# A two-layer metaformer in one kernel: weight loads one per tick, filter products partly in single PSUM banks, tokens 38 ticks behind pixels, and new orders outside full ticks

## The chip, the cores and the metric

One core of a Trainium2 chip runs the kernel. The metric is the device time of one execution in microseconds (us), the median of three runs.

## The reference

Eight images of 128 x 128 pixels with 96 channels pass two layers. A layer adds a spectral filter, then a small quantised feed-forward:

```python
x_pre = scale * relu(ln(x) @ w1.T) ** 2 + bias                 # 192 channels
xf = rfft2(x_pre)
filt = stack of 3: complex resize of cw0, cw1, cw2 to (128, 65)
r = softmax(gate(mean of x, mean of relu(bn(x @ sp_w.T))))     # per image, 3 x 192
x = x + irfft2(xf * sum_s(filt[s] * r[s])) @ w2.T
x = x + ffn(ln(x))                                             # 96 -> 384 -> 96, fp8 products
```

## The kernel before

The work is cut into 256 groups per stage (2 layers x 8 images x 16 groups) and three stages, each a generator that yields between steps: **pixels** P (norm, first product, DFT along the width, result to a_d in DRAM), **frequencies** F (read a_d, DFT along the height, filter times gate, inverse, result to y_d), **tokens** S (read y_d, last inverse DFT, add x, norm, feed-forward, write). N is the norm's small steps, U the filter products of a layer (12 groups of 8 rows, `filters`), G the gate of an image.

A loop over ticks t, from -4 on, runs a table of (stage, step, ahead): step of group t - offset + ahead. The order of a table is the order in which instructions enter each engine's queue. There are five tables: RAMP (t under 15, pixels alone), RISE (to t = 37, pixels and frequencies), TICK (full, to 257), FALL (to 275, frequencies and tokens), TAIL (tokens alone). The offset of F is 19, that of S is 40. U runs at t = 3 to 14 for layer 0 and at t = 21 to 32 for layer 1. The steps, by engine:

- P: 0 SP load xt (L526); 1 DVE st (L465); 2 POOL xn (L536); 3 PE pt_a (L540); 4 ACT xT (L543); 5 PE pw0, 10 PE pw1 (L551); 6, 11 ACT r (L554); 7, 12 ACT xs (L557); 8, 13 POOL acc (L563); 9, 14 DVE sd (L569); 15, 16 PE pa0, pa1 (L578); 17, 19 ACT lo (L592); 18, 20 DVE at (L594, L595), 20 with the store to a_d (L598).
- F: 0 SP load al, ut (L679, L681); 1 POOL ut (L685); 2, 3 PE pf0, pf1 (L697); 4 px; 5, 10 PE py0, py1 (L731); 6, 7 ACT cf (L738); 8, 11 DVE pr (L755 to L759); 9, 12 POOL xf (L774); 13, 14 PE pz (L813, L821); 15 ACT zt (L828); 16 PE pi (L837); 17 ACT yo (L840); 18 DVE yt (L844) with the store to y_d (L853).
- S: 0 SP load v, xr (L862, L865); 1 PE ps_r (L871); 2 DVE xr (L880, L882); 3 DVE st; 4, 5 xn_c on ACT and DVE (L892, L898); 6 PE pt_c (L906); 7 ACT xq; for k = 0, 1, 2: 8+4k PE pm (L916), 9+4k ACT y (L919), 10+4k DVE a (L922), 11+4k h (L926); 20 PE po (L933); 21, 22 o (L948); 23 POOL y (L951) with the store.
- U: 0 PE ps_u (L292); 1 ACT copies (L308); 2 DVE copies (L306) with the store to u_d (L311).

PSUM's eight banks are three pairs (d0, d1, d2) and two single ones (s3, s4). A BANKS table per phase says in which of them a product lies (`bank2` gives a pair, `bank1` a single); a product waits until its bank's last product has been read. All loads and stores are issued by SP, in program order. Weights are loaded and converted by events at fixed ticks, after pixel step 9: among them the layer-0 token weights (L394 to L417) at 7 and 11, layer 1's filter source cw (`load_filters`, L283) at 16, its projection weights (L334 to L369) at 19 and 23. Until t = 36 the pool `us` holds what loading needs; then the tokens' pool `sb` takes that memory.

Of the kernel before, what the change touches and what calls it, by code (L numbers as in the profile page):

```python
# [76 lines left out]
    ("F", 12, 0), ("P", 5, 0), ("P", 13, -1), ("U", 0, 0), ("U", 1, 0), ("F", 13, 0),  # L77
    ("P", 1, 2), ("P", 14, -1), ("F", 8, 1), ("P", 6, 0), ("F", 9, 1), ("P", 15, -1),
    ("U", 2, 0), ("P", 16, -1), ("P", 17, -1), ("P", 18, -1), ("F", 14, 0), ("P", 19, -1),
    ("F", 10, 1), ("P", 7, 0), ("P", 20, -1), ("F", 0, 3), ("P", 8, 0), ("F", 15, 0),  # L80
    ("N", 0, 0), ("N", 1, 0), ("P", 0, 4), ("P", 9, 0), ("F", 1, 2), ("P", 10, 0),
    ("P", 11, 0), ("N", 2, 0), ("F", 16, 0), ("F", 2, 2), ("F", 17, 0), ("F", 3, 2),
    ("P", 12, 0), ("F", 4, 2), ("F", 11, 1), ("F", 5, 2), ("P", 2, 2), ("F", 6, 2),
    ("P", 3, 2), ("F", 7, 2), ("P", 4, 2), ("F", 18, 0),
# [3 lines left out]
    1: ((7, 0), (19, 1), (19, 2), (21, 3), (21, 4), (37, 5), (43, 6)),  # L88
    2: ((15, 7), (23, 8), (23, 9), (26, 10)),
# [3 lines left out]
    ("F", 7, 1), ("F", 0, 2), ("S", 6, 0), ("S", 0, 2), ("F", 18, -1), ("S", 1, 1),  # L93
    ("S", 7, 0), ("S", 15, -1), ("S", 16, -1), ("S", 8, 0), ("F", 8, 1), ("S", 23, -3),
    ("S", 9, 0), ("S", 2, 1), ("S", 3, 1), ("N", 0, 0), ("S", 20, -2), ("S", 21, -2),
    ("S", 10, 0), ("F", 12, 0), ("F", 1, 2), ("F", 13, 0), ("F", 9, 1), ("F", 10, 1),
    ("S", 17, -1), ("N", 1, 0), ("S", 11, 0), ("S", 12, 0), ("S", 13, 0), ("F", 14, 0),
    ("F", 2, 2), ("S", 18, -1), ("N", 2, 0), ("F", 3, 2), ("F", 15, 0), ("F", 16, 0),
    ("S", 4, 1), ("S", 5, 1), ("F", 4, 2), ("F", 5, 2), ("S", 22, -2), ("F", 17, 0),
    ("F", 6, 2), ("S", 19, -1), ("F", 11, 1), ("S", 14, 0),  # L100
# [20 lines left out]
    "ps_u0": 2, "ps_u1": 0, "pa0": 0, "pa1": 2, "pw0": 1, "pw1": 2, "pt_a": 1,  # L121
# [8 lines left out]
    "ps_u0": 2, "ps_u1": 1, "ps_g": 3, "ph": 4, "pl": 3, "pa0": 2, "pa1": 0, "pw0": 0,  # L130
    "pw1": 2, "pt_a": 2, "pf0": 0, "pf1": 2, "py0": 1, "py1": 1, "pz0": 3, "pz1": 4,
    "pi0": 3, "pi1": 4, "px": 3, "pg": 4,
}
FALL_BANKS = {
    "pf0": 0, "pf1": 2, "py0": 1, "py1": 1, "pz0": 3, "pz1": 4, "pi0": 4, "pi1": 3,
    "ps_r0": 3, "ps_r1": 4, "pt_c": 0, "pm0": 1, "pm1": 2, "pm2": 2, "po": 0, "px": 4,
}
TAIL_BANKS = {
    "ps_r0": 3, "ps_r1": 4, "pt_c": 1, "pm0": 1, "pm1": 2, "pm2": 2, "po": 0,
# [100 lines left out]
def metaformer_kernel(ctx: ExitStack, tc: tile.TileContext, x, cst, layers, out):  # L240
# [44 lines left out]
    def filters(i):  # L285

        l, n0 = i // NU, i % NU * UN
        pss = []
        for i in range(2):
            pss.append(bank2(f"ps_u{i}")[:NKW, :, : UN * UM])  # L290
        for i in range(M // UM):
            mm(  # L292
                pss[i // 2][:, i % 2, :].rearrange("p (n m) -> p n m", m=UM),
                kt["rw"][32 * i : 32 * i + NWS],
                cws[l][32 * i : 32 * i + NWS, :, n0 : n0 + UN].rearrange("p m n -> p n m"),
                start=True,
                stop=True,
            )
        yield
        u = us.tile([NKW, UN, M], F32, name="u", bufs=3)  # L300
        uv = u.rearrange("p n (i a m) -> p i a n m", a=2, m=UM)
        for i, ps in enumerate(pss):
            for a in range(2):
                o = ps[:, a, :].rearrange("p (n m) -> p n m", m=UM)
                if i:
                    nc.vector.tensor_copy(uv[:, i, a], o)  # L306
                else:
                    nc.scalar.copy(uv[:, i, a], o)  # L308
            if i:
                n1 = n0 if n0 < NHS else 64 + n0 - NHS  # L310
                nc.sync.dma_start(u_d[l][:, n1 : n1 + UN, :], u)  # L311
            yield
# [7 lines left out]
    temps = [{}, {}, {}]  # L320
# [13 lines left out]
    def projection_weights(l, p):  # L334
# [26 lines left out]
        temps[l]["cen"] = cen  # L361
        ps = bank1("ps_w")
# [9 lines left out]
    def other_weights(l, p):  # L372
# [3 lines left out]
        for i in range(2):  # L376
            nc.sync.dma_start(fc1s[i * SC : (i + 1) * SC], p["conv_fc1"][C:, :])
        nc.vector.memset(kept(l, "fc1g", [C, GK]), 0.0)
        nc.vector.memset(kept(l, "fc1s", [2 * SC, GK]), 0.0)
        nc.vector.memset(kept(l, "fc2", [GK, NS * M]), 0.0)  # L380
        nc.sync.dma_start(kept(l, "mlp_s", [GK, 1]), row(p["conv_mlp_scale"], GK))
        nc.sync.dma_start(kept(l, "mlp_b", [GK, 1]), row(p["conv_mlp_bias"], GK))
        dc = kept(l, "dc", [HH, 1])
        nc.sync.dma_start(dc, row(p["conv_soa1_bias"], HH))
        nc.sync.dma_start(wt["fc2"][:RHID], p["conv_fc2"])
        yield
        ps = bank1("ps_w")
# [6 lines left out]
    def token_weights(l, p):  # L394
        wt = wts[l]


        nc.sync.dma_start(kept(l, "w2a", [128, C]), p["conv_w2"][:128, :])
        nc.sync.dma_start(kept(l, "w2c", [128, C]), p["conv_w2"][64:, :])
        w2b = kept(l, "w2b", [128, C])  # L400
        nc.sync.dma_start(w2b[:64], p["conv_w2"][128:, :])
        nc.sync.dma_start(w2b[64:], p["conv_w2"][:64, :])
        f1, f2, b1, b2 = (
            load(l, f"{name}_f", shape, view)
            for name, shape, view in (
                ("f1", [C, HID], p["ffn_W1"]),
                ("f2", [128, HID // 128, C], p["ffn_W2"].rearrange("(k p) c -> p k c", p=128)),
# [673 lines left out]
```

## Time and profile before

| | |
|---|---|
| median of three runs | 4958.87 us (4958.15 to 4959.98) |
| the profiled execution | 4954.99 us, its span 4952.9 us |
| mean granted TensorE clock | 0.986 |
| busy: PE, PEld, DVE, ACT, POOL | 97%, 76%, 93%, 87%, 51% |
| moved by DMA | 1020.95 MB, 206 GB/s |

The profile is one execution. PE is TensorE's products, PEld its weight loads beside them, DVE VectorE, ACT ScalarE, POOL GpSimd, SP the queue that issues transfers. A busy share is an average over phases with different limits, so it is read phase by phase. Waits name the releaser that came last.

### The profile page before, as it was taken

The page shows a single profiled execution, that of the slowest core. Times are in us where ns is not written, and L with a number is a line of the kernel's source. Part 1 is how long each engine was busy: PE and PEld are TensorE (multiplying, and loading weights), DVE is VectorE, ACT ScalarE, POOL GpSimd, SP SyncE. Part 2 cuts the span into 40 slices and gives each one's busy share as a digit, 9 for nine tenths or more (in the row PEclk, how much of TensorE's full clock was granted, in tenths as well). Part 3 has the DMA queues.
Part 4 walks back from the last instruction along what each step waited for, and adds up shares of the span by engine and source line. Part 5 has one row for each costly group of instructions (what it writes and reads, how often), then busy time and mean ns, then how long its engine had stood idle before and what let it go on. Part 6 is the DMA issues. An engine that isn't in the chain of part 4 may idle for free.

```text
span 4952.9 us, 123961 instructions
## 1 busy us (share of the span) xinstructions
PE 4817.7 (97%) x44232; PEld 3749.4 (76%) x44232; DVE 4587.1 (93%) x13963; ACT 4321.2 (87%) x7107; POOL 2532.7 (51%) x1889
## 2 busy tenths in 40 slices
PE   7899999999999999999999999999999999999987
PEld 4577777777777777777777787777777777777753
DVE  7777999999999999999999999999999999998888
ACT  5555799999999999999999999999999999997887
POOL 3445455555555555555555555555555555554544
PEclk9999999999999999999999999999999999999987
DMA  5677788888788888888888887888888888887754
GB/s 156 189 189 198 209 214 215 215 213 214 212 217 213 215 216 214 214 213 218 213 213 216 212 216 211 218 214 214 214 213 216 213 215 214 215 209 183 204 149 127
DMA packets 917423, 1020.95 MB, mean 206 GB/s; under 512 B 75826, under 2 KB 848914, under 8 KB 916602
## 3 DMA queue, kind: packets, MB, share of 16 engines
q1 hardware_dynamic: 916810, 1013.04, 77.2%
q8 instruction: 352, 5.77, 0.5%
q14 instruction: 261, 2.14, 0.1%
HBM read 598.92 MB, written 413.84 MB: 204 GB/s over the span
## 4 chain that ended last, share of the span: by engine, by line
PE 90%; DVE 4%; ACT 2%; issue 1%; DMA 1%; POOL 0%; SPq 0%; POOLq 0%; DVEq 0%; ACTq 0%
PE pw L551 16%; PE py L731 14%; PE pz L821 9%; PE pf L697 8%; PE pi L837 7%; PE pa L578 7%; PE pm L916 6%; PE pz L813 6%; PE po L933 5%; PE pt_a L540 4%; PE ps_r L871 4%; PE pt_c L906 2%; PE ps_u L292 1%; DVE st L465 1%; DVE xr L882 0%
## 5 line engine op out<-in xcount | busy, mean ns | idle before, releaser
L774 POOL TENSOR_TENSOR xf<-pr 128x768 f32<-128x768 f32 x512 | 931.4, 1819 | 419.4 <-DVE pr L759 409.7
L551 PE MATMUL pw<-w,xT 97*128 97x240 f32 x4096 | 943.7, 374 | 5.0 <-DVE at L595 2.9
L731 PE MATMUL py<-k_fwd,al 128*128 128x128 f32 (+1 forms) x6208 | 802.3, 280 | 0.7 <-DVE mx L637 0.4
L919 ACT CAST y<-pm 128x1024 f16<-128x1024 f32 x768 | 756.7, 1017 | 43.6 <-PE pm L916 43.4
L551 PEld LDWEIGHTS pw<-w,xT 97*128 97x128 f32 x4096 | 743.6, 191 | 58.0 <-issue 11.2
L731 PEld LDWEIGHTS py<-k_fwd,al 128*128 128x128 f32 (+1 forms) x6208 | 744.9, 191 | 41.1 <-DVE pr L759 1.7
L563 POOL TENSOR_TENSOR acc<-acc,r 128x192 f32<-128x192 f32 x496 | 296.3, 597 | 935.6 <-ACT r L554 860.9
L926 ACT ACTIVATE h<-a 128x1024 fp8e5<-128x1024 f16 x726 | 769.9, 1060 | 0.9 <-DVE a L922 0.9
L951 POOL TENSOR_TENSOR y<-xr,o 128x768 f32<-128x768 f32 x256 | 422.1, 1649 | 674.4 <-DVE o L948 582.3
L554 ACT ACTIVATE r<-pw 128x960 f32<-128x960 f32 x512 | 497.5, 972 | 115.9 <-PE pw L551 115.3
L569 DVE TENSOR_TENSOR sd<-xs 128x384 f32<-128x384 f32 x1008 | 531.9, 569 | 6.0 <-PE pa L578 5.9
L755 DVE TENSOR_TENSOR pr<-py,cf 128x768 f32<-128x768 f32 x512 | 487.0, 951 | 40.9 <-PE py L731 28.2
L685 POOL TENSOR_TENSOR ut<-ut,rw 112x768 f32<-112x768 f32 (+1 forms) x256 | 472.7, 1846 | 61.0 <-DMA ut<-u_d 42.0
L697 PEld LDWEIGHTS pf<-k_rh,ut 48*128 48x128 f32 x6080 | 362.2, 189 | 153.7 <-issue 136.3
L916 PE MATMUL pm<-xq,f_q 96*128 96x512 fp8e5 x1536 | 435.3, 391 | 40.1 <-ACT y L919 16.4
L536 POOL TENSOR_TENSOR xn_a<-xt,n_rs 128x768 f32<-128x768 f32 x256 | 378.6, 1479 | 141.2 <-DVE n_rs L499 118.5
L557 ACT ACTIVATE xs<-r 128x768 f32<-128x768 f32 x512 | 436.7, 853 | 0.4
L909 ACT ACTIVATE xq<-pt_c 96x1024 fp8e5<-96x1024 f32 x256 | 261.3, 1021 | 198.3 <-PE pt_c L906 198.3
L697 PE MATMUL pf<-k_rh,ut 48*128 48x128 f32 x6080 | 411.5, 282 | 9.7 <-POOL ut L685 9.5
L892 ACT ACTIVATE xn_c<-xr,n_nb,n_rs 128x96 fp8e5<-128x96 f32 x1062 | 414.6, 488 | 0.0
L578 PE MATMUL pa<-sd,dft 64*64 64x384 f32 x4096 | 396.8, 497 | 8.3 <-ACT r L554 4.7
L738 ACT COPY cf<-pf 128x768 f32<-128x768 f32 x496 | 373.5, 802 | 32.0 <-PE pf L697 30.3
(131 smaller groups left out, 10108.2 us busy)
## 6 DMA issues: line engine op xcount, KB each, us to landing
a_d<-at SPq DMA_DIRECT2D x256, 768.0 KB
al<-a_d SPq DMA_DIRECT2D x1024, 192.0 KB
y_d<-yt SPq DMA_DIRECT2D x512, 192.0 KB
v<-y_d SPq DMA_DIRECT2D x256, 384.0 KB
ut<-u_d SPq DMA_DIRECT2D x256, 336.0 KB
xt<-in_x_dram SPq DMA_DIRECT2D x512, 96.0 KB
xr<-in_x_dram SPq DMA_DIRECT2D x256, 192.0 KB
mid<-y SPq DMA_DIRECT2D x256, 192.0 KB
```

Of the source, the lines that this page charges most:

```text
L551: mm(o, xT[:, 4 * a + 2 * i + j, :], wt["w1"], start=True, stop=True)
L554: nc.scalar.activation(r.rearrange("p a s c -> p a (s c)"), pw, AF.Relu)
L569: on.tensor_tensor(sd[:, e], xs[:, 0], xs[:, 1], op)
L578: mm(pa[64 * e : 64 * e + 64, p].rearrange("q (s m) -> q s m", m=M), wt["dft"][64 * p : 64 * p + 64, 64 * e : 64 * e + 64], sd[64 * p : 64 ...
L685: nc.gpsimd.tensor_tensor(ut[:, -n:], ut[:, -n:], _bc_mid(jb.rw, n), ALU.mult)
L697: mm(pf[:, i, t * 128 : (t + 1) * 128], utf[64 * i : 64 * i + NHS, c0 : c0 + 128], kt["rh"][64 * i : 64 * i + NHS, :], start=True, stop=True,)
L731: mm(py[p0:p1, t, e, :], alf[:, e, c0 + p0 : c0 + p1], f, start=True, stop=True)
L755: nc.vector.tensor_tensor(p0, yv, crb, ALU.mult)
L774: nc.gpsimd.tensor_tensor(xf.rearrange("p t e f -> p (t e) f"), pr[:, 0].rearrange("p t r k -> p t (r k)"), pr[:, 1].rearrange("p t r k -> ...
L916: mm(pm[:, s, :], fk, xq[:, s, :], start=True, stop=True)
L919: nc.scalar.copy(y16, pm)
L926: nc.scalar.activation(hk, a16, AF.Copy, saturate=False)
```

## The change

The tokens' offset becomes 38, so RISE ends at t = 35, TICK runs from 36, and TAIL ends two ticks sooner. `filters` puts two of its four products into one pair (ps_u) and the others into s3 and s4 (ps_v0, ps_v1); ACT copies the first two out, DVE the others, as before. The events are replaced by one generator, `background`, of which one piece runs per tick from t = 0: one or two small loads a piece; layer 0's token weights come at 12 to 14 and are converted at 16, cw of layer 1 comes at 17, layer 1's projection weights at 18 to 21, with their small steps at 22 and their product ps_w at 23. padding(1) moves from 34 to 36. RAMP, RISE, FALL and TAIL get new orders and, in part, other banks; TICK, GATE and BANKS stay.

```diff
 RISE = (
-    ("F", 12, 0), ("P", 5, 0), ("P", 13, -1), ("U", 0, 0), ("U", 1, 0), ("F", 13, 0),
-    ("P", 1, 2), ("P", 14, -1), ("F", 8, 1), ("P", 6, 0), ("F", 9, 1), ("P", 15, -1),
-    ("U", 2, 0), ("P", 16, -1), ("P", 17, -1), ("P", 18, -1), ("F", 14, 0), ("P", 19, -1),
-    ("F", 10, 1), ("P", 7, 0), ("P", 20, -1), ("F", 0, 3), ("P", 8, 0), ("F", 15, 0),
-    ("N", 0, 0), ("N", 1, 0), ("P", 0, 4), ("P", 9, 0), ("F", 1, 2), ("P", 10, 0),
-    ("P", 11, 0), ("N", 2, 0), ("F", 16, 0), ("F", 2, 2), ("F", 17, 0), ("F", 3, 2),
-    ("P", 12, 0), ("F", 4, 2), ("F", 11, 1), ("F", 5, 2), ("P", 2, 2), ("F", 6, 2),
-    ("P", 3, 2), ("F", 7, 2), ("P", 4, 2), ("F", 18, 0),
+    ("F", 7, 1), ("P", 1, 2), ("P", 0, 3), ("P", 13, -1), ("U", 0, 0), ("F", 12, 0),
+    ("P", 3, 1), ("P", 5, 0), ("N", 0, 0), ("U", 1, 0), ("P", 4, 1), ("F", 13, 0),
+    ("U", 2, 0), ("P", 14, -1), ("P", 6, 0), ("P", 15, -1), ("F", 8, 1), ("P", 16, -1),
+    ("P", 17, -1), ("F", 14, 0), ("P", 7, 0), ("P", 18, -1), ("F", 9, 1), ("P", 8, 0),
+    ("F", 10, 1), ("P", 19, -1), ("P", 20, -1), ("N", 1, 0), ("F", 15, 0), ("F", 11, 1),
+    ("P", 9, 0), ("F", 0, 3), ("P", 10, 0), ("P", 11, 0), ("F", 16, 0), ("F", 1, 2),
+    ("F", 2, 2), ("N", 2, 0), ("F", 3, 2), ("F", 17, 0), ("P", 12, 0), ("P", 2, 2),
+    ("F", 4, 2), ("F", 5, 2), ("F", 18, 0), ("F", 6, 2),
 )
 RISE_GATE = {
-    1: ((7, 0), (19, 1), (19, 2), (21, 3), (21, 4), (37, 5), (43, 6)),
-    2: ((15, 7), (23, 8), (23, 9), (26, 10)),
+    1: ((8, 0), (25, 1), (29, 2), (37, 3), (38, 4), (42, 5), (45, 6)),
+    2: ((7, 7), (24, 8), (30, 9), (32, 10)),
 }
 FALL = (
-    ("F", 7, 1), ("F", 0, 2), ("S", 6, 0), ("S", 0, 2), ("F", 18, -1), ("S", 1, 1),
-    ("S", 7, 0), ("S", 15, -1), ("S", 16, -1), ("S", 8, 0), ("F", 8, 1), ("S", 23, -3),
-    ("S", 9, 0), ("S", 2, 1), ("S", 3, 1), ("N", 0, 0), ("S", 20, -2), ("S", 21, -2),
-    ("S", 10, 0), ("F", 12, 0), ("F", 1, 2), ("F", 13, 0), ("F", 9, 1), ("F", 10, 1),
-    ("S", 17, -1), ("N", 1, 0), ("S", 11, 0), ("S", 12, 0), ("S", 13, 0), ("F", 14, 0),
-    ("F", 2, 2), ("S", 18, -1), ("N", 2, 0), ("F", 3, 2), ("F", 15, 0), ("F", 16, 0),
-    ("S", 4, 1), ("S", 5, 1), ("F", 4, 2), ("F", 5, 2), ("S", 22, -2), ("F", 17, 0),
-    ("F", 6, 2), ("S", 19, -1), ("F", 11, 1), ("S", 14, 0),
+    ("S", 14, -1), ("F", 0, 2), ("S", 6, 0), ("F", 17, -1), ("S", 1, 1), ("S", 19, -2),
+    ("S", 0, 2), ("F", 7, 1), ("S", 7, 0), ("F", 18, -1), ("F", 8, 1), ("S", 23, -3),
+    ("S", 2, 1), ("S", 15, -1), ("F", 12, 0), ("S", 3, 1), ("N", 0, 0), ("S", 20, -2),
+    ("S", 16, -1), ("S", 8, 0), ("S", 21, -2), ("S", 9, 0), ("S", 17, -1), ("S", 10, 0),
+    ("S", 18, -1), ("F", 1, 2), ("N", 1, 0), ("F", 9, 1), ("S", 11, 0), ("S", 12, 0),
+    ("F", 13, 0), ("F", 10, 1), ("S", 13, 0), ("N", 2, 0), ("F", 14, 0), ("S", 4, 1),
+    ("F", 2, 2), ("F", 15, 0), ("S", 5, 1), ("F", 3, 2), ("F", 4, 2), ("F", 16, 0),
+    ("S", 22, -2), ("F", 11, 1), ("F", 5, 2), ("F", 6, 2),
 )
 RAMP = (
-    ("P", 0, 4), ("U", 0, 0), ("U", 1, 0), ("P", 3, 2), ("P", 20, -1), ("P", 1, 4),
-    ("P", 7, 1), ("P", 13, 0), ("P", 4, 2), ("U", 2, 0), ("N", 1, -1), ("N", 0, 0),
-    ("P", 8, 1), ("P", 14, 0), ("N", 2, -1), ("P", 2, 3), ("P", 9, 1), ("P", 10, 1),
-    ("P", 15, 0), ("P", 16, 0), ("P", 11, 1), ("P", 5, 2), ("P", 17, 0), ("P", 18, 0),
-    ("P", 19, 0), ("P", 12, 1), ("P", 6, 2),
+    ("U", 0, 0), ("P", 0, 4), ("P", 13, 0), ("U", 1, 0), ("P", 20, -1), ("P", 7, 1),
+    ("P", 1, 4), ("U", 2, 0), ("P", 3, 2), ("P", 4, 2), ("P", 8, 1), ("N", 1, -1),
+    ("P", 14, 0), ("N", 0, 0), ("N", 2, -1), ("P", 2, 3), ("P", 9, 1), ("P", 10, 1),
+    ("P", 15, 0), ("P", 11, 1), ("P", 16, 0), ("P", 17, 0), ("P", 18, 0), ("P", 19, 0),
+    ("P", 5, 2), ("P", 12, 1), ("P", 6, 2),
 )
TAIL = (
...
)
 RAMP_BANKS = {
-    "ps_u0": 2, "ps_u1": 0, "pa0": 0, "pa1": 2, "pw0": 1, "pw1": 2, "pt_a": 1,
+    "pa0": 0, "pa1": 1, "pw0": 2, "pw1": 2, "pt_a": 1, "ps_u": 0, "ps_v0": 3, "ps_v1": 4,
 }
 BANKS = {
     "ps_g": 4, "ph": 3, "pl": 4, "pa0": 1, "pa1": 0, "pw0": 0, "pw1": 0, "pt_a": 0,
     "pg": 3,
 }
 RISE_BANKS = {
-    "ps_u0": 2, "ps_u1": 1, "ps_g": 3, "ph": 4, "pl": 3, "pa0": 2, "pa1": 0, "pw0": 0,
-    "pw1": 2, "pt_a": 2, "pf0": 0, "pf1": 2, "py0": 1, "py1": 1, "pz0": 3, "pz1": 4,
-    "pi0": 3, "pi1": 4, "px": 3, "pg": 4,
+    "ps_g": 3, "ph": 3, "pl": 3, "pa0": 2, "pa1": 0, "pw0": 0, "pw1": 2, "pt_a": 2,
+    "pf0": 0, "pf1": 2, "py0": 1, "py1": 1, "pz0": 3, "pz1": 4, "pi0": 3, "pi1": 4,
+    "px": 3, "pg": 3, "ps_u": 0, "ps_v0": 3, "ps_v1": 4,
 }
 FALL_BANKS = {
-    "pf0": 0, "pf1": 2, "py0": 1, "py1": 1, "pz0": 3, "pz1": 4, "pi0": 4, "pi1": 3,
-    "ps_r0": 3, "ps_r1": 4, "pt_c": 0, "pm0": 1, "pm1": 2, "pm2": 2, "po": 0, "px": 4,
+    "pf0": 0, "pf1": 2, "py0": 1, "py1": 1, "pz0": 3, "pz1": 4, "pi0": 3, "pi1": 4,
+    "ps_r0": 3, "ps_r1": 4, "pt_c": 0, "pm0": 1, "pm1": 2, "pm2": 0, "po": 2, "px": 4,
 }
 TAIL_BANKS = {
-    "ps_r0": 3, "ps_r1": 4, "pt_c": 1, "pm0": 1, "pm1": 2, "pm2": 2, "po": 0,
+    "ps_r0": 3, "ps_r1": 4, "pt_c": 0, "pm0": 0, "pm1": 2, "pm2": 2, "po": 1,
 }
...
     def filters(i):
         l, n0 = i // NU, i % NU * UN
-        pss = []
-        for i in range(2):
-            pss.append(bank2(f"ps_u{i}")[:NKW, :, : UN * UM])
+        pu = bank2("ps_u")
+        pss = [pu[:NKW, i, : UN * UM] for i in range(2)]
+        pss += [bank1(f"ps_v{i}")[:NKW, : UN * UM] for i in range(2)]
         for i in range(M // UM):
             mm(
-                pss[i // 2][:, i % 2, :].rearrange("p (n m) -> p n m", m=UM),
+                pss[i].rearrange("p (n m) -> p n m", m=UM),
                 kt["rw"][32 * i : 32 * i + NWS],
                 cws[l][32 * i : 32 * i + NWS, :, n0 : n0 + UN].rearrange("p m n -> p n m"),
                 start=True,
             )
         yield
         u = us.tile([NKW, UN, M], F32, name="u", bufs=3)
-        uv = u.rearrange("p n (i a m) -> p i a n m", a=2, m=UM)
+        uv = u.rearrange("p n (i m) -> p i n m", m=UM)
         for i, ps in enumerate(pss):
-            for a in range(2):
-                o = ps[:, a, :].rearrange("p (n m) -> p n m", m=UM)
-                if i:
-                    nc.vector.tensor_copy(uv[:, i, a], o)
-                else:
-                    nc.scalar.copy(uv[:, i, a], o)
-            if i:
-                n1 = n0 if n0 < NHS else 64 + n0 - NHS
-                nc.sync.dma_start(u_d[l][:, n1 : n1 + UN, :], u)
-            yield
+            o = ps.rearrange("p (n m) -> p n m", m=UM)
+            if i < 2:
+                nc.scalar.copy(uv[:, i], o)
+            else:
+                nc.vector.tensor_copy(uv[:, i], o)
+            if i == 1:
+                yield
+        n1 = n0 if n0 < NHS else 64 + n0 - NHS
+        nc.sync.dma_start(u_d[l][:, n1 : n1 + UN, :], u)
+        yield
...
     def projection_weights(l, p):
...
         temps[l]["cen"] = cen
+        if l:
+            yield
         ps = bank1("ps_w")
         mm(ps[:C, :WE], cen, raw, start=True, stop=True)
...
     def token_weights(l, p):
         wt = wts[l]
-        nc.sync.dma_start(kept(l, "w2a", [128, C]), p["conv_w2"][:128, :])
-        nc.sync.dma_start(kept(l, "w2c", [128, C]), p["conv_w2"][64:, :])
...
-        f1, f2, b1, b2 = (
...
+        f1 = load(l, "f1_f", [C, HID], p["ffn_W1"])
+        yield
...
+        yield
         yield
         for name, t in (("f1", f1), ("f2", f2), ("b1", b1), ("b2", b2)):
...
-    def weights(f, l):
-
-        key = f, l
-        if key not in temps[2]:
-            temps[2][key] = f(l, layers[l])
-        return lambda: next(temps[2][key])
+    def background():
+
+        load_filters(0, layers[0])
+        constants("rw")
+        yield
+        yield from other_weights(0, layers[0])
+        for k in ("fwd", "rh"), ("inv", "rh0"), ("fwd0", "inv0"), ("idft",):
+            constants(*k)
+            yield
+        padding(0)
+        yield
+        yield from token_weights(0, layers[0])
+        load_filters(1, layers[1])
+        yield
+        yield from projection_weights(1, layers[1])
+        yield from other_weights(1, layers[1])
+        yield from token_weights(1, layers[1])
     wts, cws = [{} for _ in layers], [None for _ in layers]
     stages = {"P": pixels, "F": frequencies, "S": tokens}
-    offset = {"P": 0, "F": NRG + LAG, "S": 2 * (NRG + LAG) + 2}
-    events = {
-        0: (lambda: load_filters(0, layers[0]), lambda: constants("rw")),
-        2: (weights(other_weights, 0),),
-        5: (weights(other_weights, 0), lambda: constants("fwd", "inv")),
-        7: (weights(token_weights, 0), lambda: constants("rh", "fwd0", "rh0")),
-        9: (lambda: constants("inv0", "idft"),),
-        11: (weights(token_weights, 0),),
-        14: (lambda: padding(0),),
-        16: (lambda: load_filters(1, layers[1]),),
-        19: (weights(projection_weights, 1),),
-        23: (weights(projection_weights, 1),),
-        24: (weights(other_weights, 1),),
-        28: (weights(other_weights, 1), weights(token_weights, 1)),
-        32: (weights(token_weights, 1),),
-        34: (lambda: padding(1),),
-    }
-
+    offset = {"P": 0, "F": NRG + LAG, "S": 2 * (NRG + LAG)}
     def group(i):
         i -= UAHEAD
     with tc.manual_schedule():
         advance("P", 0, 0)
         start = projection_weights(0, layers[0])
-        next(start), next(start)
+        for _ in start:
+            pass
+        events = background()
         for t in range(-first, n + offset["S"] + behind + 1):
             norms.append(Norms())
             if t < offset["F"] - 4:
                 on_act.update(norm=NORM_ACT_TAIL, cast=CAST_ACT_TAIL, out=False)
             banks.update(places)
             if t == UEND:
+                padding(1)
                 early.close()
                 pools.append(ctx.enter_context(tc.tile_pool(name="sb", bufs=2)))
             gates = {}
                 last = i if stage == "N" else group(i) if stage == "U" else min(i, n - 1)
                 advance(stage, step, last)
                 if (stage, step) == EVENTS_AFTER:
-                    for event in events.get(t, ()):
-                        event()
+                    if t >= 0:
+                        next(events, None)
```

## The prediction

> **What bounds it.** I read the slices first, then stretches cut at whole ticks, then waits and chain where a tick is longer than its engines' work. In this page's slices each digit is a tenth of busy time:
>
> ```profile
> PE   7899999999999999999999999999999999999987
> ...
> DVE  7777999999999999999999999999999999998888
> ...
> PEclk9999999999999999999999999999999999999987
> ```
>
> PE is full but for two slices at the start and two at the end. The middle, 220 full ticks of 18.06 us (start to start of the L540 transposes, median), keeps its order in the change. So all there is to win lies outside full ticks. Stretches of whole ticks, in this order: one RAMP tick with filters, two RISE ticks without filters, two with, eight full ticks, three FALL ticks, five TAIL ticks:
>
> ```profile
> 94.60:103.60 9.00, 7.79 (x51) 4.33 (x49) 6.74 (x17) 6.39 (x12) 3.88 (x4) 1.00 0.57 156
> 472.80:501.40 28.60, 28.60 (x250) 23.70 (x249) 22.06 (x66) 17.30 (x30) 16.12 (x13) 1.00 0.82 218
> 377.60:409.40 31.80, 31.80 (x266) 23.93 (x264) 23.60 (x70) 18.60 (x34) 16.06 (x12) 1.00 0.84 210
> 1000.00:1144.50 144.50, 144.50 (x1371) 114.94 (x1369) 138.18 (x423) 132.13 (x215) 74.34 (x56) 1.00 0.82 216
> 4695.30:4735.30 40.00, 38.94 (x391) 31.14 (x390) 35.69 (x109) 35.98 (x58) 21.40 (x12) 1.00 0.82 214
> 4810.00:4850.50 40.50, 31.39 (x233) 15.18 (x231) 38.78 (x136) 35.85 (x66) 18.32 (x16) 0.79 0.50 147
> ```
>
> Columns: length, then busy PE, PEld, DVE, ACT, POOL, clock, DMA share, GB/s. Per tick: RAMP 9.0 with PE busy 7.8; RISE 14.3 or 15.9, all PE; FALL 13.33, with PE's time in one tick of the full stretch (start to start: frequencies 8.5, tokens 3.55) asking for only 12.1, and DVE 11.9 and ACT 12.0 close behind; TAIL 8.1, of which DVE is busy 7.76. In TAIL the clock is 0.79, but PE is not what it waits for.
>
> Waits over 58 to 140 us (RAMP), then over 4680 to 4748 us (FALL); columns are total, times, longest:
>
> ```profile
> DVE st L465 <- DMA xt<-in_x_dram: 8.1, 4, 4.7
> ...
> PE ps_u L292 <- DVE at L595: 4.8, 6, 1.0
> ```
> ```profile
> PEld L916 <- DVE pr L759: 3.9, 5, 0.8
> ```
>
> And the chain in RISE's tick 23, where layer 1's projection weights are made (start, length):
>
> ```profile
> 286.21 0.94 DVE sd L569 x2
> 287.14 0.11 DVE bva L350
> ...
> 289.23 0.13 DVE cen L360
> 289.36 0.14 issue
> 289.49 0.62 PE ps_w L363 x2
> 290.11 1.62 PE pw L551 x8
> ```
>
> PE stands with pw queued behind ps_w, which waits for a chain of small DVE and ACT steps.
>
> **The sum, against the profiled execution (4954.99 us, span 4952.9; the median of the runs, 4958.87, is 3.9 above it).**
>
> *Two ticks less lag.* Work is unchanged; two more ticks are full, RISE loses two ticks without filters, TAIL loses two: 2 x (18.06 - 14.3 - 8.1) = -8.7. This needs no order to be better.
>
> *RAMP's 12 filter ticks.* The built order of PE, ACT and POOL is the same as before in such a tick; only sd and the norm's first step swap on DVE. The banks differ. Before, ps_u0 lay with pa1 and ps_u1 with pa0, so L292 waited for both pairs of at (0.9 us per tick, the row above). Now ps_u lies with pa0 alone and ps_v in single banks that RAMP otherwise leaves free: the second pair of at (2 x 0.47) no longer stands before it. What is late next is DVE: st 1.3, u 0.94, two sd 0.94 and 1.7, norm 1.4, at 1.9, together 8.2 with waits of 0.2 or 0.3 that I see no reason to vanish. I take 8.5 for 9.0: -6. Ends: 0, and PE's own 7.8, -14. One wait is added: pt_a now lies with pa1, so it waits for the second pair of at, and pw is queued behind it. The 1.43 us of ps_u cover these 0.94. In the five ticks before the first filters that cover is gone, but there pt_a waited for r of pw0 instead (its old bank mate). 0, at most +4.
>
> A rule on the clock bears on this. The granted clock is 0.92 over 58 to 140 us, with no PE wait of more than 1.4 us listed outside the loads' ticks. The Trainium skill (TensorE: Matmul & The Clock Gate, Part 1) says that the gate closes only after an idle window of about 3.4 us. By the rule shorter waits cost no clock and removing them returns none; by the row, a full clock would give 0.08 x 7.8 x 12 = -7 more. I take none, since DVE, not PE, is what I expect to bound these ticks.
>
> *Bursts of loads in RAMP.* Tick 8 took 12.7 and tick 11 11.6. Tick 7 issues 11 loads at once, each some 0.61 us of SP (L853's median is 614 ns), so 6.8 us stand before the xt loads that st waits for: the 4.7 above. The skill's page DMA: Bandwidth & Descriptors (Issuing engines are not separate DMA queues) calls issue time usually small beside the transfer, and its Rules for kernel authors count transfers under 64 KB as mostly overhead. By that rule spreading saves nothing, since as many transfers remain; by the row it saves the 3.7 over 9.0, because SP's 6.8 us are split over ticks in which it idles. I go by the row: -3.5. Tick 11's 2.6 are the conversions on DVE (L414, 2.2 us). They go to tick 16, where DVE also holds the first image's gate, and the second half of the gate queues behind them; 0 to -2.6, I take -1. Together -4.5, ends 0 and -6.3.
>
> *Start of RISE.* Layer 1's cw (1.9 MB) is issued at 188 us, and the second group's ut lands at 209: 5.7 MB in 28 us with DMA 84 to 94% busy, PE idle up to 6.6 us at a time. The load moves to tick 17, right before that group's al and ut on SP, behind xt. The bytes ahead of ut remain, less one xt (0.38 MB, 2 us). -2; -6 if the first group's ut, now with nothing behind it, lands sooner, +4 if cw stands in front longer.
>
> *Loads in RISE.* Tick 23 is 3.1 over 15.9, tick 25 1.7 over. A yield now stands between the DVE chain and ps_w, so ps_w finds its input. But the chain sits in tick 22 on DVE, waiting for two ACT steps behind zt; behind it are n_a and yt. DVE is busy 74% there, which hides it; without that cover 1 to 2 us. -3, ends 0 and -4.8. RISE's new order itself: PE is full there. 0, ends -3 and +3.
>
> *FALL, 17 steady ticks.* Two stalls show: pm0 (in py0's bank) waits 0.8 for pr, and pz spends 1.55 instead of 1.07 because it shares banks with ps_r, which xr is still reading. In the new order po and pm2 (1.4 us) stand between ps_r and pm0, po no longer lies with pf0 and pt_c, and pz comes 26 places after ps_r instead of 16. New: ps_r's second half waits for yt, whose yo heads ACT's tick; behind it pt_c's successors wait. I take 12.85 for 13.33, between none and PE's 12.1, as three engines near 12 rarely interlock fully: -8; ends 0 and -21.
>
> *TAIL.* DVE does 7.76 of 8.1; half of the rest over 18 ticks is -3, ends 0 and -6. po, a tick later per group, lengthens the very end by about its 1 us: +1.
>
> *The v loads.* y_d's last part was issued 45 us before v's first; two ticks less leave 9. A landing took 3.3 us (a_d at 178) to 13.8 (behind cw). If it takes longer than 9, SP holds xr, a_d and xt; v is read 1.4 ticks (25 us) later and xt a tick later, so 0. Likewise padding(1), now in tick 36 just before the token pool takes that memory: one wait of up to 5.
>
> Sum: -8.7 - 6 - 4.5 - 2 - 3 - 8 - 3 + 1 = -34.2. 4958.9 - 34 gives **4925**.
>
> **Rivals.**
> - *Only what needs no overlap pays.* The lag, the bursts and tick 23 come, the waits that go in FALL and RAMP return as others, since DVE and ACT are busy 90% in FALL. -8.7 - 4.5 - 3 = -16: 4943. For it: three engines at 12.0 of 13.3.
> - *The floors are reached.* FALL 12.4, RAMP 8.1, TAIL 7.8: -8.7 - 11 - 5 - 3 - 4 - 16 - 5 = -53: 4906. For it: each stall above has a named bank behind it that is changed.
> - *Slower: single banks tie PE to DVE in RISE.* ps_v lies with pz and pi. L292's last product now waits for yt, and pz waits for the two DVE copies of u, behind st and the norm; pa and py queue behind pz. DVE needs 4.1 us from yt to the copies' end, PE has 7.0 us between pi and pz (pf, py, ps_u, pt_a, pw). Each us that DVE is later than that margin of 2.9 costs 12. It decides against the change from 3.7 us of stall per tick (44 in all): about 4972. Against it: DVE idles 8 of 31.8 us there.
>
> **From this to chances.** Main case 0.65, first rival 0.18, floors 0.13, slower 0.04. A measurement can tell 0.2% (9.9 us) from no change. About a third of the first rival lies within it. Faster 0.90, same 0.06, slower 0.04. Range 4905 to 4948: the floors' time below; above, the first rival and somewhat over it. The unknown costs all at their bad ends would give 4965, all at their good ends 4892.
>
> **What would show it.** Right: full ticks stay 18.06; FALL 12.6 to 13.0; RAMP filter ticks 8.3 to 8.7 without PE ps_u waiting for at L595; ticks 8, 11, 23 near their neighbours; TAIL under 8.0; 12 RISE ticks with filters at 15.6 to 16. Wrong: SP waiting for y_d before v, pz waiting for copies of u, pm waiting for pr as before, a longer gap at 180 to 215 us, or full ticks that differ, for then the lag's arithmetic fails.

## The result and the profile after

The changed kernel takes 4929.3 us (median of six runs, 4927.91 to 4936.49); the kernel before, on the same chip, 4959.06 (six runs, 4956.68 to 4964.09). The ratio is 0.9942, with a 95% interval of 0.9929 to 0.9955: 28.8 us less, 22 to 35. The prediction was 4925. The profiled execution took 4929.2, span 4927.4, clock 0.986, 25.8 less than the profiled one of before. From line 400 or so on, a line of before is 18 further down after (L526 is L544, L569 is L587, L813 is L831).

The slices of after:

```profile
PE   7899999999999999999999999999999999999987
...
DVE  7788999999999999999999999999999999998998
...
PEclk9899999999999999999999999999999999999997
```

PE fills the same slices as before, and its clock still dips only at both ends. What changed is too small for slices. So again stretches of whole ticks (columns as before: length, then busy PE, PEld, DVE, ACT, POOL, clock, DMA share, GB/s): a RAMP tick with filters, two RISE ticks without, two with, eight full ticks, four FALL ticks, five TAIL ticks:

```profile
95.60:102.90 7.30, 7.30 (x52) 4.41 (x48) 6.20 (x23) 6.29 (x12) 3.18 (x3) 1.00 0.69 226
448.30:477.10 28.80, 28.80 (x250) 23.77 (x250) 25.73 (x71) 16.86 (x30) 16.05 (x12) 1.00 0.67 190
366.90:399.30 32.40, 32.40 (x271) 24.46 (x268) 26.51 (x70) 18.88 (x36) 15.89 (x12) 1.00 0.70 193
1000.00:1144.50 144.50, 144.50 (x1351) 114.56 (x1349) 138.16 (x423) 132.03 (x214) 75.13 (x56) 1.00 0.79 217
4680.00:4731.20 51.20, 50.74 (x512) 39.74 (x510) 47.69 (x145) 46.50 (x76) 28.46 (x16) 1.00 0.77 216
4782.10:4822.60 40.50, 30.52 (x231) 16.22 (x230) 38.79 (x136) 35.80 (x66) 19.72 (x15) 0.83 0.50 148
```

Full ticks stay at 18.06. RAMP's clean tick fell from 9.0 to 7.3, with PE busy all of it (before 7.8 of 9.0). FALL's is 12.8 where nothing disturbs it (mean of 15 ticks 12.93, before 13.35). TAIL's stays 8.1, and RISE's tick with filters went up, from 15.9 to 16.1 or 16.2.

The waits that the prediction named, in RAMP (58 to 140 us) and then in FALL (4668 to 4736 us), as total, times, longest:

```profile
DVE st L483 <- DMA xt<-in_x_dram: 14.0, 9, 4.9
...
PE ps_u L292 <- DVE at L613: 1.2, 2, 0.8
```
```profile
PEld L934 <- issue: 1.9, 5, 0.4
```

PE's wait for `at` is nearly gone (4.8 before), and pm no longer waits for pr. But st waits longer for its pixels: 14.0 us for 8.1.

The chain at tick 23, where the projection weights were made:

```profile
276.39 1.37 PE py L749 x12
277.75 0.41 PE ps_w L368 x2
278.16 1.62 PE pw L569 x8
```

ps_w follows py with nothing in between, as foreseen.

Where the time went by phase, read from the start times of the same groups in both profiles. The prediction's terms are put to the same borders; a negative number is a gain:

| stretch | predicted | after | loads alone | RAMP's places alone | lag alone |
|---|---|---|---|---|---|
| RAMP, to pixel group 16 | -10.5 | -13.9 | -6.0 | -8.3 | +0.6 |
| from there to the first pz | -2 | +3.1 | -8.2 | -0.2 | +1.7 |
| RISE, 16 groups | -3 | +0.8 | -0.3 | 0.0 | -0.1 |
| switch to full ticks, to pz 22 | +7.5 | +9.1 | 0.0 | 0.0 | +10.7 |
| full ticks, to pz 238 | 0 | +0.4 | +1.9 | -0.1 | +1.3 |
| FALL, to the last pz | -8 | -6.0 | +0.5 | -0.9 | +0.2 |
| TAIL and end | -18.2 | -19.0 | +1.6 | +2.2 | -14.9 |
| sum | -34.2 | -25.5 | -10.5 | -7.3 | -0.5 |

One execution is one sample: six executions that run the same code up to group 16 (after and five of the kernels below) stand there at -13.9, -13.6, -13.0, -11.8, -9.2 and -7.5. So RAMP is known to some 3 us, and the totals of single profiles with it; verdicts on whole parts come from the runs' ratios. Steady ticks repeat to 0.1 us.

Two stretches went against the forecast. At the start of RISE, SyncE's queue in 176 to 204 us (start, time from the first issue to the end of the last, number of transfers):

```profile
176.90 0.32 SPq L616 DMA_DIRECT2D a_d<-at  x1
177.32 3.09 SPq L283 DMA_DIRECT2D cw<-in_L_cw_dram  x4
180.46 2.66 SPq L697 DMA_DIRECT2D al<-a_d  x4
184.88 1.97 SPq L699 DMA_DIRECT2D ut<-u_d  x1
187.56 7.32 SPq L544 DMA_DIRECT2D xt<-in_x_dram  x4
```

and what waited in 165 to 212 us:

```profile
POOL ut L703 <- DMA ut<-u_d: 10.3, 1, 10.3
```

The 1.9 MB of cw are issued in front of al, ut and xt; four issues of xt then take 7.3 us, and POOL stands 10.3 us for ut, PE behind it.

In RAMP, tick 12 (127.5 to 141.8 us) takes 14.3 us. The chain there begins with loads of pixels:

```profile
127.09 4.61 DMA xt<-in_x_dram
...
131.79 0.26 DVE st L483
```

SyncE's queue ahead of that tick:

```profile
122.82 0.37 SPq L317 DMA_DIRECT2D u_d<-pad  x1
123.28 5.88 SPq L544 DMA_DIRECT2D xt<-in_x_dram  x4
```

The padding store of layer 0 (0.8 MB) is issued right ahead of the pixel loads, whose four issues then take 5.9 us. The window of that tick:

```profile
127.50:141.80 14.30, 10.42 (x53) 5.91 (x49) 8.11 (x33) 6.32 (x12) 4.43 (x6) 0.74 0.67 224
```

PE stands 3.9 us, and its products then take 3.1 us more than in a clean tick, at a clock of 0.74: nearly half of the 7 us is clock. Before, that store stood at tick 14 (166 us), where it met the switch to RISE.

One single tick went the same way: RISE's tick 32, before first:

```profile
429.34:446.13 16.79, 16.27 (x147) 13.39 (x143) 12.35 (x44) 9.27 (x17) 6.44 (x6) 1.00 0.49 132
```
```profile
418.16:436.42 18.26, 17.79 (x144) 15.05 (x143) 14.20 (x41) 8.73 (x16) 7.75 (x7) 0.91 0.65 171
```

The clock was at half for 3.4 us of it, which makes the 1.5 us. All nine profiles here with the new RISE have this step; it begins 0.8 to 1.9 us after a wait of PE of only 0.47 us for a small step of the image's gate (hm); none of the five with the old RISE has it. Why the new order brings it was not tried.

### The profile page after: what moved, and what is told of

The parts are those of the page before. It is cut to its first block, busy times and chain, and to the rows that moved or that the text cites. A ratio compares the mean times of both kernels' runs of the same rounds, so it can differ in the third digit from the quotient of the medians.

```text
span 4927.4 us, 124008 instructions
## 1 busy us (share of the span) xinstructions
PE 4813.4 (98%) x44232; PEld 3751.1 (76%) x44232; DVE 4592.9 (93%) x13949; ACT 4311.3 (87%) x7104; POOL 2532.6 (51%) x1886
## 4 chain that ended last, share of the span: by engine, by line
PE 88%; DVE 5%; ACT 4%; issue 1%; DMA 1%; SPq 1%; POOL 0%; POOLq 0%; DVEq 0%; ACTq 0%
PE pw L569 16%; PE py L749 14%; PE pz L839 8%; PE pf L715 7%; PE pa L596 7%; PE pi L855 7%; PE pm L934 6%; PE pz L831 5%; PE po L951 5%; PE pt_a L558 4%; PE ps_r L889 4%; PE pt_c L924 2%; DVE st L483 1%; ACT y L937 1%; ACT xn_c L910 1%
## 5 line engine op out<-in xcount | busy, mean ns | idle before, releaser
L569 PE MATMUL pw<-w,xT 97*128 97x240 f32 x4096 | 944.3, 374 | 7.4 <-DVE at L613 2.9
L569 PEld LDWEIGHTS pw<-w,xT 97*128 97x128 f32 x4096 | 742.5, 191 | 61.6 <-ACT r L572 7.4
L587 DVE TENSOR_TENSOR sd<-xs 128x384 f32<-128x384 f32 x1008 | 518.7, 554 | 1.7 <-PE pa L596 1.4
L756 ACT COPY cf<-pf 128x768 f32<-128x768 f32 x496 | 372.7, 801 | 33.6 <-PE pf L715 33.2
```

The lines of the kernel that those rows point to most:

```text
L569: mm(o, xT[:, 4 * a + 2 * i + j, :], wt["w1"], start=True, stop=True)
L587: on.tensor_tensor(sd[:, e], xs[:, 0], xs[:, 1], op)
```

## The experiments

Times below are medians; each ratio is to runs of the kernel before on the same chip, with its 95% interval.

**The order of RAMP alone, or the PSUM places alone.** In the profile after I saw that one DVE step sd (a sum or difference of xs; the expectations below wrongly call it a division) takes 0.55 us in most ticks instead of 1.76, since it starts ahead of POOL's xn. I took the new order for the cause. Two kernels part order and places.

```diff
 # order alone: the kernel before, with
-RAMP = (("P", 0, 4), ("U", 0, 0), ("U", 1, 0), ...)
+RAMP = (("U", 0, 0), ("P", 0, 4), ("P", 13, 0), ...)
```
```diff
 # places alone: the kernel before, with
 RAMP_BANKS = {
-    "ps_u0": 2, "ps_u1": 0, "pa0": 0, "pa1": 2, "pw0": 1, "pw1": 2, "pt_a": 1,
+    "pa0": 0, "pa1": 1, "pw0": 2, "pw1": 2, "pt_a": 1, "ps_u": 0, "ps_v0": 3, "ps_v1": 4,
+# and the new copies of u, in RAMP only
```

> The kernel before with the new order of RAMP alone; PSUM places, copies, loads and lag as before. Theory: the first division of a tick takes about 0.6 us instead of 1.8, clean filter ticks fall to 7.3 to 7.8 us, and RAMP is some 12 us shorter, total about 4946. Rival (order without the single banks leaves TensorE to wait for the pair's second copy): filter ticks 8.3 to 9 us, total 4953 to 4958.

> The kernel before with the new PSUM places and the new copies of the filter products in RAMP alone; orders, loads and lag as before. Theory (the order is what shortens the filter ticks, because it lets VectorE's division start ahead of GpSimd's step): clean filter ticks stay at 8.8 to 9.0 us and the division stays at about 1.8 us; total within 3 us of before. Rival (the single banks remove VectorE's waits): clean filter ticks fall to about 7.3 to 8 us, RAMP is 12 to 16 us shorter, total about 4944.

Order alone: 4959.85 us, 0.9998 (0.9989 to 1.0006). Places alone: 4951.09, 0.9982 (0.9974 to 0.9990), -8.9 us. One clean RAMP tick of each, order alone first:

```profile
85.46:94.49 9.03, 7.81 (x52) 4.35 (x48) 8.03 (x25) 6.39 (x12) 3.89 (x4) 1.00 0.55 177
```
```profile
66.31:73.64 7.33, 7.33 (x52) 4.44 (x49) 6.50 (x25) 6.28 (x12) 3.86 (x5) 1.00 0.64 206
```

My theory fell: the rival of the places gives the whole 1.7 us. The DVE and POOL rows of these ticks (start, length) show what sd does in each, order alone first:

```profile
89.29 1.77 DVE L569 TENSOR_TENSOR sd<-xs 128x384 f32<-128x384 f32 x1 [0.20 <-PE pa L578]
```
```profile
89.18 1.47 POOL L536 TENSOR_TENSOR xn_a<-xt,n_rs 128x768 f32<-128x768 f32 x1 [4.16 <-DVE n_rs L499]
```
```profile
69.96 0.56 DVE L575 TENSOR_TENSOR sd<-xs 128x384 f32<-128x384 f32 x1
```
```profile
70.09 1.75 POOL L542 TENSOR_TENSOR xn_a<-xt,n_rs 128x768 f32<-128x768 f32 x1 [3.33 <-DVE n_rs L505]
```

With the old places sd waits 0.2 us for PE's pa, starts 0.11 behind xn, and ends 0.4 after it. With the new places it need not wait, starts 0.13 ahead, and xn pays 0.28 instead. So the wait that the places remove moves sd to the other side of xn, and sd is 1.2 us shorter. No kernel parts the clash from the bank wait, but tick 13 of the next kernel (the loads alone, old order, old places) happens to: its sd starts 0.16 us ahead of xn and takes 0.55.

```profile
150.31:158.37 8.06, 7.75 (x53) 4.33 (x49) 6.83 (x27) 6.39 (x12) 3.55 (x5) 1.00 0.67 215
```

It takes 8.06 us, where that kernel's ticks 8 to 11, with the clash, take 9.02. By this tick about 1.0 of the 1.7 us is the clash and 0.7 is left for the wait. It is one tick, right behind one that a store stretched, so this is a sign and no proof.

**The spread of loads alone**, on the kernel before.

```diff
-    events = {0: (lambda: load_filters(0, layers[0]), ...), 2: ..., 34: ...}
+    events = background()
```

> The kernel before with the new spread of weight loads, and the padding stores at ticks 11 and 36, alone; orders, PSUM places, copies and lag as before. As the prediction had it, this part is worth 4.5 in RAMP, 2 at the start of RISE and 3 in RISE: about 4950. Theory now (the lag took 10, the places of RAMP 9 and the order of FALL 7 of the 30, so little is left for the loads, because the padding store and the 1.9 MB load stand in front of pixel loads): 4956 to 4960.

4945.44 us, 0.9974 (0.9964 to 0.9984), -12.9 us. The theory that little was left for the loads fell; the prediction's 9.5 was near. RAMP's ticks 8 and 11 are 9.0 instead of 12.7 and 11.6, and the store at tick 11 costs about 1 us (a tick of 10.2), where it costs 7 with ticks of 7.3. At the start of RISE this kernel gains 8.2. Its SyncE queue there:

```profile
184.45 1.42 SPq L699 DMA_DIRECT2D ut<-u_d  x1
185.97 2.50 SPq L544 DMA_DIRECT2D xt<-in_x_dram  x4
188.82 3.79 SPq L283 DMA_DIRECT2D cw<-in_L_cw_dram  x4
196.79 0.35 SPq L616 DMA_DIRECT2D a_d<-at  x1
```

In the old RISE table frequency step 0 and pixel step 0 stand before pixel step 9, after which events run; in the new one frequency step 0 stands behind it. So the same event issues cw behind ut and xt here, and in front of them after. The two kernels also differ in lag and in RAMP; that one step's position was not tried alone.

**cw in four loads**, on the changed kernel.

```diff
-        load_filters(1, layers[1])
-        yield
-        yield from projection_weights(1, layers[1])
+        cws[1] = us.tile([128, UM, NG], F32, name="cw")
+        rest = projection_weights(1, layers[1])
+        for i in range(M // UM):
+            nc.sync.dma_start(cws[1][32 * i : 32 * i + NWS], layers[1]["cw"][:, i * UM : (i + 1) * UM, :])
+            if i:
+                next(rest)
+            yield
+        yield from rest
```

> The changed kernel with layer 1's filter parameters (1.9 MB in one load at tick 17) in four loads over ticks 17 to 20, beside the projection loads. Theory (the burst in front of the pixel loads costs the 3 to 5 us that the start of RISE lost): the tick of 22.9 us falls to 17 or less, the first product of RISE comes some 4 to 8 us earlier, total 4921 to 4925. Rival (the start of RISE is bound by the bytes that have to land there, as the padding store that only moved its stall suggests): ticks 17 to 22 take the same 78 us in sum, total within 2 us of 4929.

4921.43 us (4918.92 to 4924.54), 0.9925 (0.9910 to 0.9940). That is 7.9 below the changed kernel's median, and no run of one reaches a run of the other, though the intervals of the ratios overlap: it is the better of the two. The longest tick at the start of RISE, after first, then here:

```profile
182.50:205.40 22.90, 13.07 (x90) 10.75 (x89) 14.12 (x32) 7.29 (x12) 7.91 (x6) 0.72 0.89 207
```
```profile
181.80:197.70 15.90, 13.10 (x90) 10.77 (x90) 14.13 (x33) 7.29 (x12) 8.39 (x6) 0.82 0.83 193
```

The same work, 7 us less of standing. The stretch from group 16 to the first pz goes from +3.1 to -4.7.

**The padding store elsewhere**: at tick 14; in four pieces at ticks 11 to 14; on ScalarE's queue. The last two have cw in four loads as well.

```diff
 # at tick 14 (in four pieces: padding(0, part) at each of four ticks)
-        padding(0)
-        yield
-        yield from token_weights(0, layers[0])
+        for i, _ in enumerate(token_weights(0, layers[0])):
+            if i == 3:
+                padding(0)
+            yield
+        yield
```
```diff
 # on ScalarE's queue
-        nc.sync.dma_start(dst, _bc_mid(pad, 4))
+        queue = nc.sync if l else nc.scalar
+        queue.dma_start(dst, _bc_mid(pad, 4))
```

> The changed kernel with layer 0's padding store (0.8 MB) issued at tick 14 instead of 11, the token loads one tick earlier in its place. Theory: the tick of 14.2 us in RAMP falls to 7.5 to 9, the store then lies beside the switch from RAMP to RISE where it costs nothing, RAMP is about 6 us shorter and the whole about 4923. Rival (whichever transfer of 0.8 MB stands ahead of the pixel loads costs the same): the stall moves to tick 14 or 15 and the total stays within 2 us of 4929.

> The changed kernel with the filter parameters of layer 1 in four loads (as in the run before, which gave 4921.4) and layer 0's padding store in four pieces of 0.2 MB at ticks 11 to 14. Theory (a large transfer straight in front of the pixel loads is what stalls them, not the bytes in sum): the tick of 13.6 us in RAMP falls to 8 to 9.5, nothing comes back at the switch, total about 4916 to 4918. Rival (these bytes cost the same wherever they are put, as when the whole store was moved): ticks 11 to 18 keep their sum, total within 2 us of 4921.4.

> The same (filter parameters in four loads), with layer 0's padding store whole at tick 11, but issued from ScalarE's queue instead of SyncE's. Theory (pixel loads stand behind it in one queue; on a queue of its own they pass it): the tick of 13.6 us falls to 8 to 10, total about 4916 to 4918. Rival (the engines that move the data are shared, so the pixel loads are as late as before): the tick stays above 12 us, total within 2 us of 4921.4.

At tick 14: 4929.97 us, 0.9937 (0.9920 to 0.9953). In pieces: 4920.92 (four runs, 4915.1 to 4931.4), 0.9926 (0.9911 to 0.9940). On ScalarE's queue: 4922.64, 0.9927 (0.9912 to 0.9942). None gains over its base (4929.3, 4921.4, 4921.4) by more than the noise; the rival was right three times. With the store at tick 14, tick 12 falls to 8.5 us, but tick 14 stretches, from 7.2:

```profile
147.30:160.10 12.80, 8.95 (x43) 5.61 (x42) 8.46 (x31) 6.52 (x14) 4.40 (x6) 0.70 0.66 203
```

In pieces tick 12 is 8.7, and ticks 14 and 15 are 11.6 and 12.3 (in its base, cw in four loads: 7.2 and 9.6). On ScalarE's queue tick 12 stays 14.4, and the pixel loads on SyncE's are as slow:

```profile
126.17 5.89 SPq L552 DMA_DIRECT2D xt<-in_x_dram  x4
```

The four issues take 5.9 us as before, although nothing large stands ahead of them on their own queue; with the store moved to tick 14 the same four took 3.8. So it isn't their queue's order that holds them here. Up to pixel group 18 these three stand at -9.2, -8.3 and -8.3 against before, after and the kernel with cw in four loads at -11.9 and -12.4; that is within the spread of one execution, and shows no gain. Bytes that must land in these ticks cost about the same wherever I put them. At the start of RISE, for cw, the place did matter.

**The lag alone, and padding(1) earlier.** In the profile after, the first full tick is 19.4 us (before 17.8), and the chain there runs through padding(1). One kernel has the lag of 38 and nothing else (its store is at tick 34); the other is the changed kernel with that store at tick 33.

```diff
-    offset = {"P": 0, "F": NRG + LAG, "S": 2 * (NRG + LAG) + 2}
+    offset = {"P": 0, "F": NRG + LAG, "S": 2 * (NRG + LAG)}
```
```diff
+            if t == 33:
+                padding(1)
             if t == UEND:
-                padding(1)
```

> The kernel before with the token lag of 38 alone. Theory: two pure full ticks of 18.06 us replace two FALL ticks of about 13.3 and one TAIL pair and so on as the prediction worked it: -8.7 us in all, so about 4950; from the first product of RISE to the first full tick the offset against before grows by about 7.5 us, and RAMP, the tick lengths of RISE, FALL and TAIL stay as before. Rival (the handoff itself costs about 3 us more, whoever makes it): about 4953, with the first full tick some 10.7 us later against before, as in the changed kernel. If the 3 us belong to the padding store of layer 1, they do not show here, because that store is still at tick 34.

> The changed kernel with layer 1's padding store at tick 33 instead of 36, so that it lands before the first load of the filter products needs it. Theory (the load waits for that store, as the chain of waits shows): the tick of 19.4 us falls to about 17.8, total about 4926 to 4928. Rival (the kernel with the lag alone, whose store is at tick 34, loses the same 3 us there): the tick stays at 19 or more, total within 1 us of 4929.

Lag alone: 4950.01 us (13 runs), 0.9980 (0.9972 to 0.9988), -9.9 us against the -8.7 worked out; the later first full tick (+10.7 in the table) is the rival's. Padding earlier: 4930.15, 0.9942 (0.9928 to 0.9957): nothing. There the store is out of the chain, and the tick is still 21.0. The windows of that tick tell why. In order: the kernel with the store on ScalarE's queue, the changed kernel, the one with padding(1) earlier, the one with cw in four loads:

```profile
488.90:506.80 17.90, 16.07 (x144) 12.64 (x142) 16.81 (x50) 10.55 (x20) 8.05 (x6) 1.00 0.77 209
```
```profile
494.70:514.10 19.40, 17.57 (x141) 13.18 (x140) 16.75 (x50) 10.49 (x20) 8.06 (x6) 0.91 0.76 211
```
```profile
496.10:517.10 21.00, 19.17 (x143) 14.76 (x142) 16.94 (x50) 10.64 (x20) 8.05 (x6) 0.84 0.73 205
```
```profile
487.20:509.80 22.60, 20.79 (x141) 16.27 (x140) 17.83 (x52) 10.88 (x20) 8.10 (x6) 0.77 0.81 229
```

The clock column alone orders them. Length times one minus clock is 0, 1.7, 3.4 and 5.2 us, and the ticks are 17.9 plus nearly that. Besides transfers that were long done by then, the first and the third differ in the padding and the clock, and it is the one with the early padding that is slower; the first has padding(1) at tick 36, as after. So padding(1)'s wait costs nothing that shows, and the lost time is TensorE's clock. PE's rows of the first and the last of the four (start, length, operation, and idle time before it):

```profile
499.79 1.86 PE L577 MATMUL pw<-w,xT 97*128 97x240 f32 x8 [1.83 <-DVE at L621]
...
502.39 1.61 PE L723 MATMUL pf<-k_rh,ut 48*128 48x128 f32 x24
```
```profile
498.01 2.55 PE L576 MATMUL pw<-w,xT 97*128 97x240 f32 x8 [1.81 <-DVE at L620]
...
501.98 2.93 PE L722 MATMUL pf<-k_rh,ut 48*128 48x128 f32 x24
```

After the same idle time pw takes 1.86 us in one and 2.55 in the other, and pf, two products later, 1.61 and 2.93. This wait of 1.8 us is in all 14 profiles of this document. Half clock follows it in nine of the ten with the lag of 38, and in none of the four with the lag of 40 (before, the order alone, RAMP's places alone, the loads alone). So the loss comes with the lag; by what, stays open.

**FALL of before, whole, or its places alone; TAIL of before**, each put back in the changed kernel.

```diff
 FALL_BANKS = {
-    ... "pi0": 3, "pi1": 4, ... "pm2": 0, "po": 2, "px": 4,
+    ... "pi0": 4, "pi1": 3, ... "pm2": 2, "po": 0, "px": 4,
```

> The changed kernel with the order and the PSUM places of FALL of before. Theory: FALL's ticks go back from 12.8 to 13.3 us, 17 ticks, so about +6 to +8: 4935 to 4937. Rival (FALL's ticks were shortened by something that comes with the lag): the ticks stay at 12.8 and the total within 2 us of 4929.

> The changed kernel with the PSUM places of FALL of before, its new order kept. With both of before the total was 4936.2. Theory (the places, which let a product start before another's bank is read out, made FALL's ticks shorter): most of the 7 us comes back, total 4934 to 4936, ticks of 13.2 to 13.3 us. Rival (the order did it): ticks stay at 12.8, total within 2 us of 4929.3.

> The changed kernel with the order and the PSUM places of TAIL of before. Theory: TAIL stays bound by VectorE at 8.1 us a tick either way, so the total stays within 2 us of 4929. Rival (as the prediction had it, the order is worth about 3): TAIL's ticks go to 8.2, total 4932.

FALL of before: 4936.21 us, 0.9956 (0.9942 to 0.9971), ticks of 13.34 again; so FALL is worth about 7. TAIL of before: 4933.12, 0.9948 (0.9932 to 0.9965), ticks of 8.1 either way, so the ticks are the theory's and the total is the rival's. The ranges of these runs and of the changed kernel's overlap; in the profile the switch from FALL to TAIL is some 2 us longer. Places of before with the new order: 4988.16, 1.0058 (1.0041 to 1.0075), far slower than either expectation. Three ticks of its FALL, and a wait there that neither before nor after lists (4680 to 4748 us):

```profile
4681.10:4729.90 48.80, 41.68 (x394) 34.16 (x394) 35.22 (x101) 34.84 (x55) 20.09 (x12) 0.91 0.60 167
```
```profile
PE pm L934 <- ACT y L937: 6.0, 3, 2.0
```

Ticks of 16.3: pm2 shares a bank with pm1 and waits until ACT has read it, 2.0 us or a little more in each tick. The clock of 0.91 adds some 1.5 us a tick, and 12.8, 2.0 and 1.5 make the 16.3. So the new order needs these places: without them it is 52 us slower than FALL of before. The new places with the old order were not run, so their own worth stays open.

## Why the prediction was right, and where it was not

The total was right to 4 us, and most parts have the right sign. Single terms were off by more, and some of that cancels. The prediction also started from the median, 3.9 above the profiled execution. Redone, its sums of bad and good ends come to about 4967 and 4890, not 4965 and 4892, which changes nothing.

- *Lag, -8.7*: right. Alone it gives -9.9 (6 to 14). In the profiled executions part went back to the clock at the switch, 1.6 us after and about 3.2 with the lag alone; the term had nothing for that, though nine of ten profiles with this lag show it.
- *RAMP's filter ticks, -6*: right cause, wrong size. The places did it, by the wait that the prediction named, and alone give -8.9. The failed step is "DVE is late next, 8.2 with waits that I see no reason to vanish": those 8 us held a clash of 1.2 between sd and xn, which is no work and went with the wait. DVE is then busy 6.2. PE's "7.8" was no floor either: with the new places its products take 7.3. Twelve ticks at 1.7 would be -20; slower ticks with loads, and the padding store's, took the rest back. The five ticks before the first filters, put at 0 to +4, gained 3.2.
- *The clock in RAMP*: over 58 to 140 us it rose from 0.92 to 0.97, but clean ticks had 1.00 in both kernels, so it explains none of the 1.7. In RISE and at the switch the Trainium skill's rule (TensorE: Matmul & The Clock Gate, Part 1: the gate closes only after an idle window of about 3.4 us) doesn't hold: half clock followed a wait of 0.47 us in tick 32, and one of 1.8 us in the first full tick of nine profiles. After the wait of 3.9 us in tick 12 the clock fell, as the rule says.
- *Bursts in RAMP, -4.5*: the row was the better guide than the skill's remark that issue time is "usually small relative to the DMA itself" (DMA: Bandwidth & Descriptors, Issuing engines are not separate DMA queues). With the old order and places tick 8 gives back its 3.7, tick 11 its 2.6 (put at 1), and RAMP 6.0. The spread moves the loads' bytes together with their issues, so which of the two counted isn't parted. The step that was missing is the padding store: with ticks of 7.3 us, 0.8 MB make one tick 14.3. The prediction priced only layer 1's store.
- *Start of RISE, -2*: wrong, +3.1, near the end that I had named as "+4 if cw stands in front longer". The failed step is "the bytes ahead of ut remain, less one xt". What counts is what stands ahead on SyncE. The loads alone gain 8.2 there; in the whole change this is a loss, by the queue's rows because the new RISE puts cw in front; cw in four loads gains 7.8 back. It is also where the parts don't add: lag, places, loads and FALL alone come to -9.9, -8.9, -12.9 and -7, in sum -39 (-43 with TAIL's 4), and the change is -29; 11 of the gap are between +3.1 and -8.2.
- *Loads in RISE, -3, and order, 0*: +0.8 together. Tick 23 fell from 19.0 to 16.5, but tick 22 grew by 1.1, where the small steps on DVE and ACT now hold r, and tick 32 takes 18.3 for 16.8, by the clock. The loads alone don't do it: there ticks 22 and 23 take 35.1 together, 34.9 before and 33.6 after. The new RISE costs 0.2 us in each of 12 ticks; with the old RISE (loads alone, lag alone, RAMP's places alone) they stay at 15.9. Which of its places or steps does it wasn't tried. It may be a small form of the slow rival, well inside its margin.
- *padding(1) and v, 0*: right; the chain runs through the store, and its removal gives nothing. Of SP's waits there (455 to 520 us) none is for y_d.
- *FALL, -8*: right, -6.0 in the profile and 7 in the runs, ticks 12.8 to 12.9 for 12.85 predicted. The prediction took places and order as separate helps; the order without the places is 52 us slower than FALL of before.
- *TAIL, -3, end +1*: about right in size, wrong in place. The tick stays 8.1, DVE's own; about 2 us come at the switch.

## What to carry to other kernels

When an engine is called the bound, take waiting out of its busy time first: compare each operation's duration with the same operation elsewhere, as sd's 1.76 against 0.55. Parts that make a phase faster take away the slack in which transfers hid, so price every transfer at the new tick length and at its new place in the queue, against the loads that stand behind it. An order and its memory places are one change; half of it can cost seven times what the whole gains, as in FALL.

## What the runs showed of the hardware

- TensorE's clock fell to half in steps of some 3.4 us, each worth about 1.6 us where PE is the bound, after waits well under 3.4 us: after one of 0.47 us in tick 32 in nine of nine profiles with the new RISE, after one of 1.8 us in nine of ten with the lag of 38. In tick 32 it fell in none of the five with the old RISE; in the first full tick in none of the four with the lag of 40, though they have the wait of 1.8 us too. In one tick this makes 17.9 to 22.6 us.
- A DVE operation of 0.55 us (sd) that starts 0.12 us after a POOL operation of 1.47 (xn) lasts 1.75 to 1.77, past the other's end (17 pairs in RAMP of before, the order alone and the loads alone). Started 0.16 us before it, it lasts 0.55 or 0.56, and the POOL operation 1.72.
- A store of 0.8 MB on ScalarE's queue held up the pixel loads on SyncE's as much as one on SyncE's own: four issues took 5.89 and 5.88 us, and 3.75 with the store moved away.
